# A two-layer image kernel: layer 1's pools open behind the last scan, its first steps between those of the last image's end, and the mixing made one round ahead

## The chip, the cores and the metric

The kernel runs as one launch on one core of one Trainium2 chip. The metric is the device time of the launch in microseconds (us), lower is better. Engines are called as the profile calls them: PE is TensorE (PEld its weight loads), DVE is VectorE, ACT is ScalarE, POOL is GpSimd, and SP is SyncE, which here only issues DMAs.

## The reference, cut to what matters

The input `x` is 4 images of 48 x 48 x 128 in float32. Two residual layers follow each other.

```
layer 0, per image:  xz = in_proj(group_norm(x));  xin, z = split(xz)
    xc = silu(conv3x3_depthwise(xin))                     # d = 256
    xs = [xc, xc transposed, both reversed]               # 4 directions, L = 2304
    dt, B, C = projections of xs
    h[l] = h[l-1] * exp(dt*A) + dt*u*B[l];  y[l] = h[l]*C[l]   # 16 states
    x1 = x + out_proj(layer_norm(sum of directions) * silu(z))

layer 1:  xa = instance_norm(group_norm(x1))              # (b, t): 48 x 128 pictures
    k, q, v = spectral convolutions of xa, 32 heads
    attn = softmax(q . k over t, s);  out = attn . v
    proj = spectral convolution of out + skip;  attention = inorm(proj + xa)
    m = two spectral layers of attention (gelu in the first)
    result = x1 + inorm(m) + attention
```

A spectral convolution takes the FFT of a picture, multiplies a few modes by complex weights and transforms back. The kernel does the transforms as matmuls with fixed matrices, and it works on the attention in the modes: the scores come from the transformed pictures, and the attention weights are applied to transformed pictures too ("mixing").

## The kernel before

**Two ways to place an instruction.** What is called through `on.` is kept in program order (all of it has line L55 in the profile, the line of the helper). What is called through `nc.` is placed by a scheduler on its engine, as early as its data, its memory and the order allow. Either way each engine then runs its instructions strictly in order.

**Layer 0** (`first_layer`) goes over image `b`, direction `k` in the order 0, 2, 1, 3, chunks of 480 of 2304 positions, and 16 state steps in each chunk. A step has matmuls that spread its factors (`da`, `pb`), the scan `h` on DVE, the product `hc` with the C rows `cbc` on POOL, and the matmul `yp` that sums over states. `advance` interleaves the stages of neighbouring steps; the C rows are fetched by SP four steps ahead. Everything else (projections, convolution, the end of a chunk) is written as generators in the queue `later`, of which `piece()` runs one step per `advance`. The end of a chunk is `gather`, then `back`: products `pg`, layer norm (`pm`, `yb`, `pv`, `var`, `pe`), gate (`pz0`, `pz1`, `ws`), output projection (`po`), residual (`pr`), and a store to `x1_dram`. All matmuls of `back` use one PSUM bank (`side`), so they form a serial chain. After the last step of the last image the rest of `later` runs alone:

```
    for _ in range(len(window)):
        advance(None)
    while later:
        piece()
```

**Layer 1** (`layer1`) starts when `io["first"]` has returned. It loads all four images back from `x1_dram` (`x_in`, L1000), as two pairs of images. Then:

- `prepare()` fills `qs` with zeros and builds the selection matrices `sel` (memsets and copies on POOL).
- For each pair `p`: `statistics` (`bn_stats` `st`, `mv`, and `group_affine`: `gm_l`, `gv_l`, one power `aff` on POOL), then `first_norm` (means `pm`, `po_m`; four centrings to `xa`; squares `sq`; `pv`, `po_v`; `in_r`) in turn with `forward_w`, the transform along w (`pfwb`, and six steps of two matmuls `pa` with their evacuations `a`).
- Weights of the heads: `gw` on DVE, transposes `pgt`, stored as `dgt`. Then the normalised pictures transposed (`pxn`, `xnt`), the modes of q and k selected (`psel`), and products `ps` for the modes that carry no weight (`s0`).
- Scores, per pair: twelve steps `jn` of 8 matmuls `sc` with a product `f` on DVE or POOL, then 8 matmuls `s0 . d_qk`. Beside them `keys()` makes transposed pictures, one image (48 rows) at a time: `pxt`, `xt`, stored as `dxt`. After each pair the softmax over its scores (`mx`, `s`, `sm`, `sn`), its transposes `pat` and a copy to `attn_c`.
- Mixing: 96 rounds, `k` (4) x pair (2) x `q` (3) x `g` (4). SP fetches `xrep` (two transfers of 576 KB for every four rounds, two buffers) and `grep` (576 KB, 16 in all). A round is `gp` (ACT copy, L1624), `v` on DVE (L1626), `v` on POOL (L1630) and 12 matmuls `acc` (L1634) into three PSUM banks. After twelve rounds the sums go out: one ACT copy, three DVE operations to `zt` (L1645 to L1647), and two transposes `pz` to `z2`. After the second quarter `mix_of_images` adds 24 matmuls `pa` per pair (L1570).

The rest (`Strand`, phases `p0` to `p5`, two pairs in turn) is the output projection, the two spectral layers and the result.

Of the kernel before, what the change touches and what calls it, by code (L numbers as in the profile page):

```python
# [10 lines left out]
F32 = mybir.dt.float32  # L11
# [47 lines left out]
def first_layer(ctx, tc, io, x1_dram, sp_dram, d_w, d_m):  # L59
# [14 lines left out]
    four = ctx.enter_context(tc.tile_pool(name="l0_four", bufs=4))  # L74
    ring = ctx.enter_context(tc.tile_pool(name="l0_ring", bufs=RING))
    ps_a = ctx.enter_context(tc.tile_pool(name="l0_psa", bufs=1, space=PSUM))
# [3 lines left out]
    rows = ctx.enter_context(tc.tile_pool(name="l0_rows", bufs=ROWS))  # L80
    dram = ctx.enter_context(tc.tile_pool(name="l0_dram", bufs=8, space=DRAM))

# [403 lines left out]
    def back(b, s, n, yb, x, w, wb):  # L486
# [66 lines left out]
        for f in range(NF):  # L553
            on.tensor.matmul(pr[:, 0:n], w_out[:, 1, f], z[:, f, 0:n], start=False, stop=(f == NF - 1))
        yield
        on.vector.tensor_add(xo[:, 0:n], xo[:, 0:n], pr[:, 0:n])
        last = b == B - 1 and s == 0
        (nc.scalar if last else nc.sync).dma_start(
            x1_dram[b].rearrange("w h t -> w (h t)")[:, s : s + n], xo[:, 0:n]
        )  # L560
# [313 lines left out]

    turns = deque(maxlen=2)
# [8 lines left out]
    for j, chunks in enumerate(directions):  # L884
# [3 lines left out]
        if k == ORDER[-1]:  # L888
            drain(coming)
            images[b]["x"] = load_x(b, "xr")  # L890
        nxt = upcoming(j + 1) if j + 1 < len(directions) else None
# [37 lines left out]
    while later:  # L929
        piece()  # L930
# [32 lines left out]
def layer1(ctx, tc, io, x1_dram, out):  # L963
# [11 lines left out]
    io["first"](sp_d, d_w, d_m)  # L975

    imgs = ctx.enter_context(tc.tile_pool(name="l1_imgs", bufs=1, side="right"))
    const = ctx.enter_context(tc.tile_pool(name="l1_const", bufs=1, side="right"))
    small = ctx.enter_context(tc.tile_pool(name="l1_small", bufs=2, side="right"))
    on = Ordered(tc)  # L980
    img = ctx.enter_context(tc.tile_pool(name="l1_img", bufs=1))

    def load(name, shape, src, eng=nc.sync):
        t = const.tile(shape, F32, name=name)
        eng.dma_start(t, src)
        return t
# [3 lines left out]

    xa = img.tile([128, H, BT], F32, name="xa")
    ident = load("ident1", [128, 128], io["c_ident"])
    fh = load("fh", [96, 96], io["c_FH"])
    x_in = [imgs.tile([128, 2, H, T], F32, tag=f"p{p}", name=f"x_in{p}") for p in range(2)]
    for b in range(B):

        for s, n in CHUNKS if b == B - 1 else [(0, L)]:
            h = slice(s // T, (s + n) // T)
            last = b == B - 1 and s == 0
            (nc.scalar if last else nc.sync).dma_start(x_in[b // 2][:, b % 2, h], x1_dram[b][:, h])  # L1000
    gmat = load("gmat1", [128, 128], io["c_group"])
    fw = load("fw", [128, 66], io["c_FW"])
    eps = const.tile([128, 1], F32, name="eps1")
    nc.gpsimd.memset(eps, 1e-5)
    half = const.tile([128, 1], F32, name="half1")
    nc.gpsimd.memset(half, -0.5)
    mean_m = const.tile([128, 32], F32, name="mean_m")
    nc.gpsimd.memset(mean_m, 1.0 / (H * W))
    over_h = const.tile([H, H], F32, name="over_h")
    nc.gpsimd.memset(over_h, 1.0 / H)  # L1010
    over_w = const.tile([128, T], F32, name="over_w")
    nc.gpsimd.memset(over_w, 1.0 / W)

    g_of = const.tile([128, 2, 128], F32, name="g_of")
    nc.gpsimd.memset(g_of, 0.0)
    for b in range(2):
        nc.gpsimd.memset(g_of[64 * b : 64 * b + 64, b], 1.0 / 32)
    n_g = everywhere("n_g", io["L1_norm_g"], 6)
    n_b = everywhere("n_b", io["L1_norm_b"], 6)
    HB = 8  # L1020
# [10 lines left out]
    def statistics(psum, p, x):  # L1031

        mv = small.tile([128, 2, 2], F32, tag=f"mv{p}", name=f"mv{p}", bufs=1)
        for b in range(2):
            st = small.tile([128, 6, 6], F32, tag="st", name=f"st1_{p}_{b}")
            for q in range(6):
                on.vector.bn_stats(st[:, q], x[:, b, q * HB : (q + 1) * HB].rearrange("p h t -> p (h t)"))
            on.vector.bn_aggr(mv[:, b], st)
        aff = small.tile([128, 2, 2], F32, tag=f"aff{p}", name=f"aff{p}", bufs=1)
        group_affine(on, small, psum, gmat, half, mv[:, :, 0], mv[:, :, 1], aff[:, 0], aff[:, 1], 2, f"l1{p}")  # L1040
        return aff
# [28 lines left out]
    def first_norm(psum, work, p, x, aff, y):  # L1070

        a_m = small.tile([128, 2], F32, tag="a_m", name=f"a_m{p}")
        on.vector.tensor_scalar(a_m, aff[:, 0], 1.0 / (H * W), None, ALU.mult)
        quarters = [(2 * b + i, b, 24 * i) for b in range(2) for i in range(2)]

        def spread(t, name, more=False):

            v = small.tile([128, T], F32, tag="in_s", name=f"in_{name}{p}")  # L1080
            on.vector.tensor_reduce(v, t[:, 0 : HB * T].rearrange("p (h t) -> p t h", t=T), AX.X, ALU.add)
            o = psum.tile([128, 512], F32, tag="st", name=f"po_{name}{p}", bufs=2)
            for b in range(2):
                ob = o[:, b * T : (b + 1) * T]
                on.tensor.matmul(ob, g_of[:, b], v, start=True, stop=not more)
                if more:
                    on.tensor.matmul(
                        ob, aff[:, 1, b : b + 1].to_broadcast([128, 128]), over_w, start=False, stop=True
                    )
            return o  # L1090

        pm = psum.tile([128, 512], F32, tag="st", name=f"pm{p}", bufs=2)
# [9 lines left out]
        yield  # L1102
        om = spread(pm, "m", True)
# [5 lines left out]
        yield  # L1109
        pv = psum.tile([128, 512], F32, tag="st", name=f"pv{p}", bufs=2)  # L1110
        for i, b, h in quarters:
            d = y[:, h : h + 24, p * 96 + b * T : p * 96 + (b + 1) * T]
            on.vector.scalar_tensor_tensor(
                d,
                x[:, b, h : h + 24],
                aff[:, 0, b : b + 1],
                m[:, b, None, :].to_broadcast([128, 24, T]),
                ALU.mult,
                ALU.add,
            )  # L1120
            sq = work.tile([128, 24, T], F32, tag="sq", name=f"sq{p}_{i}")
# [7 lines left out]
        ov = spread(pv, "v")  # L1129
        r = small.tile([128, 96], F32, tag=f"in_r{p}", name=f"in_r{p}", bufs=1)  # L1130
# [3 lines left out]
        yield r  # L1134

# [7 lines left out]
    a0_bd = const.tile([96, 2, 96], F32, name="a0_bd")  # L1143
    zp = ctx.enter_context(tc.tile_pool(name="l1_z", bufs=1))
# [17 lines left out]
    nc.vector.tensor_mul(wpv[:, 0], wpv[:, 0], wpv[:, 1])  # L1162
    dxt = dram.tile([B, 4, T, 3 * NC], F32, name="dxt")
# [12 lines left out]
    s0 = pe.tile([T, B, T], F32, name="s0")  # L1176
# [38 lines left out]
    def products():  # L1215
        cqk = pe.tile([T, NH], F32, name="cqk")
# [4 lines left out]
        with ExitStack() as pw:  # L1221
# [19 lines left out]
            nc.scalar.copy(n_col, pn[:, 0:4].rearrange("p (s z) -> p s z", z=2))  # L1241

# [59 lines left out]
    with ExitStack() as ph:  # L1302
        psum = ph.enter_context(tc.tile_pool(name="l1_ps0", bufs=3, space=PSUM))
        psst = ph.enter_context(tc.tile_pool(name="l1_ps0s", bufs=1, space=PSUM))
        work = ph.enter_context(tc.tile_pool(name="l1_work0", bufs=2))
        prepare()
        rs, das = [], []
        for p in range(2):
            aff = statistics(psst, p, x_in[p])
            norm = first_norm(psst, work, p, x_in[p], aff, xa)  # L1310
            trans = forward_w(psum, work, p, x_in[p], aff)
            next(norm)
            next(trans)
            next(norm)
            for _ in range(5):
                next(trans)
                next(norm)
            das.append(next(trans))
            rs.append(next(norm))
        with ExitStack() as pw:  # L1320
            ps_t = pw.enter_context(tc.tile_pool(name="l1_wt", bufs=2, space=PSUM))
            q1 = pw.enter_context(tc.tile_pool(name="l1_w1", bufs=1, side="right"))
# [4 lines left out]
            for c in range(2):  # L1327
                nc.sync.dma_start(w_p[:, :, c], io["wP"][c].rearrange("(j p) h -> p j h", p=128))
                nc.sync.dma_start(w_v[:, :, c], io["wV"][c].rearrange("(j p) h -> p j h", p=128))
                nc.sync.dma_start(d48[c], io[("c_D48r", "c_D48i")[c]])  # L1330
            for c in range(2):
                p = ps_t.tile([128, 512], F32, tag="tr", name=f"pv48{c}")
                on.tensor.matmul(p[:, 0:NH], d48[c], w_v[:, 0, c], start=True, stop=True)
                on.scalar.copy(w_v[:, 0, c], p[:, 0:NH])
            gw = q1.tile([128, 12, 3, NH], F32, name="gw")
# [14 lines left out]

            for k in range(4):
# [6 lines left out]
                nc.sync.dma_start(dgt[k], gt.rearrange("h c n -> h (c n)"))  # L1358
        pl = ph.enter_context(tc.tile_pool(name="l1_plain", bufs=1))
# [4 lines left out]
        b48 = small.tile([128, 1], F32, tag="b48", name="b48")  # L1364
        on.vector.tensor_scalar(b48, n_b[:, 0:1], 1.0 / H, None, ALU.mult)
        one1 = small.tile([1, 1], F32, tag="one1", name="one1_x")
        nc.gpsimd.memset(one1, 1.0)
        pr = psst.tile([128, 512], F32, tag="pp", name="pr0")
        r_t = small.tile([96, 2], F32, tag="r_t", name="r_t")
# [63 lines left out]
        u32 = const.tile([24, BT], F32, name="u32")  # L1433
# [783 lines left out]
```

## Time and profile before

| | |
|---|---|
| median of 3 runs | 4521.48 us (4520.93 to 4522.82) |
| profiled execution | 4536.64 us, span 4534.9 us, mean PE clock 0.936 |
| PE busy | 3854.2 us (85%) |
| DVE busy | 3854.3 us (85%) |
| ACT busy | 3439.2 us (76%) |
| POOL busy | 3356.7 us (74%) |
| layer 0, last product `hc` starts | 3709.43 us |
| end of the last chunk | 3747.4 us |
| pair 0's norm and transform, first `pm` | 3771.87 us |
| pair 1's norm and transform, first `pm` | 3808.72 us |
| scores | 3889.9 to 3993.6 us |
| mixing, first and last `acc` | 4021.8 to 4262.6 us |
| `Strand`, first matmul `pe_p` | 4269.83 us |

Starts are microseconds from the start of the span. The page divides the span into 40 slices of 113 us, each digit the busy share of an engine in tenths; PEclk is the clock that the throttle granted to PE. A line of the chain of waits is start, length, engine, operation and line, or the transfer or the "issue" time that the chain went through. In the timeline an operation's line ends with the idle time before it and what released it. The windows give, for a stretch, the busy time of PE, PEld, DVE, ACT and POOL with counts, then the PE clock, the share of the DMA engines and GB/s.

### The profile page before, as it was taken

How to read it: one execution, taken by the hardware profiler on the slowest of the kernel's cores; microseconds unless marked ns; L12 is line 12 of the kernel's file. 1: busy time of each engine (PE TensorE's matmuls, PEld its weight loads, DVE VectorE, ACT ScalarE, POOL GpSimd, SP SyncE). 2: the span in 40 equal slices, each digit the busy share in tenths (PEclk: the TensorE clock that was granted, in tenths of full speed). 3: DMA queues.
4: the chain of work that ended last, by engine and by line, in shares of the span. 5: the costliest groups of instructions: out<-in, count | busy, mean ns of one | idle time of the engine just before them, and what ended most of it. 6: DMA issues, size and time to landing. Idle time of an engine off the chain costs nothing.

```text
span 4534.9 us, 73722 instructions
## 1 busy us (share of the span) xinstructions
PE 3854.2 (85%) x26212; PEld 2993.0 (66%) x26212; DVE 3854.3 (85%) x2646; ACT 3439.2 (76%) x6964; POOL 3356.7 (74%) x3523
## 2 busy tenths in 40 slices
PE   6989987888899878888998788878877885979877
PEld 3777776777777767776777677767776762535444
DVE  3888999999899999998999999989999974657446
ACT  3888888988888889887888899879998862323344
POOL 2777788988787889887878898978888961356432
PEclk9989999999999899998999999999999997989877
DMA  2333333333333333333333333434333332155536
GB/s 63 93 94 103 91 100 100 111 96 110 97 106 94 96 102 111 98 110 94 107 93 96 103 107 100 115 94 111 104 105 105 100 111 62 25 128 138 133 101 160
DMA packets 327068, 461.05 MB, mean 102 GB/s; under 512 B 112788, under 2 KB 295636, under 8 KB 325996
## 3 DMA queue, kind: packets, MB, share of 16 engines
q1 hardware_dynamic: 311904, 433.20, 35.0%
q10 hardware_dynamic: 14796, 23.13, 1.5%
q8 instruction: 208, 3.41, 0.3%
q14 instruction: 160, 1.31, 0.1%
HBM read 400.99 MB, written 55.44 MB: 101 GB/s over the span
## 4 chain that ended last, share of the span: by engine, by line
PE 35%; ACT 22%; DVE 21%; issue 12%; POOL 5%; DMA 3%; SPq 1%; ACTq 0%; DVEq 0%; POOLq 0%
DVE h L55 13%; PE yp L55 8%; ACT scaled L55 6%; PE pc L55 5%; DVE db L55 4%; ACT da L55 4%; PE da L55 4%; ACT decay L55 4%; PE pd L55 2%; POOL hc L55 2%; PE acc L1634 2%; ACT dt L55 2%; ACT turned L55 2%; PE pg L55 2%; PE pb L55 2%
## 5 line engine op out<-in xcount | busy, mean ns | idle before, releaser
L55 POOL TENSOR_TENSOR hc<-h,cbc 128x960 f32<-128x960 f32 (+1 forms) x1280 | 2546.1, 1991 | 565.4 <-PE yp L55 194.1
L55 DVE TENSOR_TENSOR_SCAN h<-da,carry,db 128x962 f32<-128x962 f32 (+1 forms) x640 | 1355.9, 2119 | 115.7 <-ACT da L55 97.3
L55 DVE TENSOR_TENSOR_SCAN h<-decay,carry,da 128x962 f32<-128x962 f32 (+1 forms) x640 | 1362.5, 2129 | 6.5 <-PE da L55 6.2
L55 PE MATMUL yp<-ident,hc 128*128 128x128 f32 (+1 forms) x9728 | 1268.6, 283 | 52.9 <-POOL hc L55 49.3
L55 PEld LDWEIGHTS yp<-ident,hc 128*128 128x128 f32 (+1 forms) x9728 | 1140.6, 145 | 217.5 <-issue 109.3
L55 ACT ACTIVATE scaled<-turned,bt 128x256 f32<-128x256 f32 (+1 forms) x2432 | 1035.5, 497 | 27.5 <-ACT turned L55 23.6
L55 ACT ACTIVATE da<-dt,a_neg 128x480 f32<-128x480 f32 (+1 forms) x1280 | 826.1, 645 | 187.9 <-DVE h L55 165.0
L55 ACT ACTIVATE decay<-dt,a_neg 128x480 f32<-128x480 f32 (+1 forms) x1280 | 799.1, 674 | 28.2 <-DVE h L55 23.6
L55 PE MATMUL da<-ident,scaled 128*128 128x128 f32 (+1 forms) x4864 | 646.5, 276 | 194.1 <-DVE h L55 178.5
L55 DVE TENSOR_TENSOR db<-du,pb 128x960 f32<-128x960 f32 (+1 forms) x640 | 699.0, 1092 | 110.1 <-PE pb L55 100.1
L55 PEld LDWEIGHTS da<-ident,scaled 128*128 128x128 f32 (+1 forms) x4864 | 543.8, 145 | 243.0 <-ACT scaled L55 97.9
L55 PE MATMUL pb<-ident,bt 128*128 128x128 f32 (+1 forms) x2432 | 376.6, 276 | 38.4 <-DVE db L55 38.4
L55 PEld LDWEIGHTS pb<-ident,bt 128*128 128x128 f32 (+1 forms) x2432 | 292.7, 141 | 171.4 <-issue 98.2
L55 PE MATMUL pc<-pad,w_c 128*128 128x480 f32 (+1 forms) x720 | 335.9, 581 | 6.5 <-ACT th L55 3.0
L55 POOL TENSOR_TENSOR du<-dt,xc 128x480 f32<-128x480 f32 (+1 forms) x160 | 206.4, 1290 | 49.5 <-ACT dt L55 49.5
L1630 POOL TENSOR_TENSOR v<-grep,xrep 128x768 f32<-128x768 f32 x96 | 174.8, 1823 | 89.8 <-PE acc L1634 47.5
L1634 PE MATMUL acc<-v,attn_c 128*64 128x384 f32 x1152 | 211.1, 502 | 29.4 <-DVE v L1626 15.3
L1626 DVE TENSOR_TENSOR v<-gp,xrep 128x1536 f32<-128x1536 f32 x96 | 167.7, 1756 | 76.4 <-PE acc L1634 43.9
L55 PEld LDWEIGHTS da<-carry,ident 128*128 128x128 f32 x1280 | 201.6, 199 | 0.0
L55 PE MATMUL da<-carry,ident 128*128 128x2 f32 x1280 | 197.6, 224 | 0.0
L55 POOL COPY carry<-h 128x2 f32<-128x2 f32 x1024 | 194.9, 190 | 0.0
L1634 PEld LDWEIGHTS acc<-v,attn_c 128*64 128x64 f32 x1152 | 113.2, 139 | 116.8 <-issue 63.6
(382 smaller groups left out, 3995.9 us busy)
## 6 DMA issues: line engine op xcount, KB each, us to landing
cbc<-cd SPq DMA_DIRECT2D x512, 240.0 KB
cbc<-other SPq DMA_DIRECT2D x512, 240.0 KB
xrep<-dxt SPq DMA_DIRECT2D x48, 576.0 KB
cbc<-cd SPq DMA_DIRECT2D x128, 192.0 KB
cbc<-other SPq DMA_DIRECT2D x128, 192.0 KB
yt<-turned ACTq DMA_DIRECT2D x40, 384.0 KB
old<-yt SPq DMA_DIRECT2D x40, 384.0 KB
grep<-dgt SPq DMA_DIRECT2D x16, 576.0 KB
```

The costliest lines, as they stand in the source:

```text
L55: return lambda *args, **kw: self._tc.keep_in_program_order(emit(*args, **kw))
L1626: nc.vector.tensor_mul(v, gp[:, None, :, 0:NC].to_broadcast([128, 2, 2, NC]), x[:, :, 0:2])
L1630: nc.gpsimd.tensor_mul(v3, r[:, 2:3].to_broadcast([128, 2, NC]), x[:, :, 2])
L1634: nc.tensor.matmul(acc[c][64 * b : 64 * b + 64, 0:NC], attn_c[:, 2 * pair + b, g, q], v[:, b, c] if c < 2 else v3[:, b], start=first, stop ...
```

## The change

1. **Pools.** In layer 0, the pools `four`, `ring`, `rows` and `ps_a` are opened last and closed behind the last step (`scans.close()`). A new function `opening` opens layer 1's first pools there, its matmuls with one PSUM bank per tag (`pp`, `mm`, `st`).
2. **Images 0 and 1 between the steps of the end.** `return_x` loads images 0 and 1 once more into an `xc` buffer (`x_0`, eight loads of 288 KB), queued at the last image's last direction; in the built order they stand in SP's queue in image 2's last direction. Then one step of `opening` follows each piece of the last chunk's end: statistics, affine, means, transform and squares of pair 0, on `x_0`. In the built order the squares, half of the transform and the statistics of the third image come after the last piece.
3. **Last chunk's result** is added straight into `x_in[1]`, and its store goes by SP.
4. **Order behind it.** `pow` for pair 1 and its norm and transform follow; the centring of pair 0 into `xa` comes later, between the steps of the weights of the heads. `prepare()` stands later in the source; in the built order its POOL instructions stand behind the last `pv` and square of `x_0` (whose memory `qs` takes) and ahead of pair 1's `pow`. `iw2`, `fw64` and `ih` are loaded here and not after the mixing.
5. **Scores.** `keys()` takes both images of a pair (96 rows): 16 groups `pxt` in all instead of 32, all in pair 0's scores. `s0 . d_qk` comes first. The softmax is split: `open_soft` (maxima, subtraction, exponential) right behind a pair's scores; `close_soft` of pair 0 during pair 1's scores, of pair 1 around the first mixing rounds. The `xrep` of the first two steps is fetched during pair 1's scores.
6. **Mixing.** `make(n + 1)` (the copy and the products) stands before `use(n)` (the matmuls). Three ACT copies take the sums out; the DVE operations and the `pz` of a group follow in the next rounds. `grep` fetches are spread. The mix of images becomes 24 matmuls of 96 columns at the end, multiplied by a mask `own`.

The diff, cut to its core:

```diff
+    scans = ctx.enter_context(ExitStack())
+    four = scans.enter_context(tc.tile_pool(name="l0_four", bufs=4))
+    ring = scans.enter_context(tc.tile_pool(name="l0_ring", bufs=RING))
+    rows = scans.enter_context(tc.tile_pool(name="l0_rows", bufs=ROWS))
+    ps_a = scans.enter_context(tc.tile_pool(name="l0_psa", bufs=1, space=PSUM))
...
+        to = xo[:, 0:n]
+        if b == B - 1 and s == 0:
+            to = images[b]["x1"][:, 1].rearrange("w h t -> w (h t)")[:, 0:n]
+        on.vector.tensor_add(to, xo[:, 0:n], pr[:, 0:n])
+        nc.sync.dma_start(x1_dram[b].rearrange("w h t -> w (h t)")[:, s : s + n], to)
...
+    def return_x(x):
+        for i in range(NF):
+            for q in range(0, L, 576):
+                nc.sync.dma_start(x[:, i, q : q + 576], x1_dram[i].rearrange("w h t -> w (h t)")[:, q : q + 576])
+                yield FREE
...
-    while later:
-        piece()
+    scans.close()
+    with ExitStack() as tail:
+        beside = opening(tail, x_0.rearrange("p b (h t) -> p b h t", t=T), images[B - 1])
+        next(beside)
+        while later:
+            piece()
+            next(beside, None)
+        images[B - 1]["done"] = True
+        for _ in beside:
+            pass
...
+    def opening(stack, x_0, last):
...
+        measure(0, 0, x_0, range(6))
+        yield
+        measure(0, 1, x_0, range(6))
+        yield
+        made["aff"] = [affine(psum, 0)]
+        yield
+        trans = forward_w(psum, work, 0, x_0, made["aff"][0])
+        norm = means(psum, 0, x_0, made["aff"][0])
+        for _ in range(3):
+            next(norm)
+            yield
+        made["m"] = next(norm)
+        for i in range(H // HB):
+            next(trans)
+            yield
+        made["da"] = [next(trans)]
+        rest = squares(psum, None, 0, x_0, made["aff"][0], made["m"])
+        for i in range(5):
+            next(rest)
+            yield
+            if i == 1:
+                measure(1, 0, x_in[1], range(6))
+        made["r"] = [next(rest)]
+        measure(1, 1, x_in[1], range(2, 6))
...
+        while "done" not in last:
+            yield
+        measure(1, 1, x_in[1], range(2))
+        made["aff"].append(affine(psum, 1))
...
+                for _ in range(2 * (pair == 0 and jn % 3 != 2)):
+                    next(beside, None)
+                if pair and jn == 1:
+                    for i in range(2):
+                        fetch(i, ahead[:, i])
+                if pair and jn % 2 and jn < 8:
+                    close_soft(0, jn // 2)
+            for _ in beside:
+                pass
+            open_soft(pair, sc)
...
+            for g in range(4):
+                fetch_weights(0, g)
+            for g in range(2):
+                close_soft(1, g)
+            make(0)
+            for n in range(len(rounds)):
+                if n < 2:
+                    close_soft(1, 2 + n)
+                if n + 1 < len(rounds):
+                    make(n + 1)
+                todo = after.popleft() if after else None
+                use(n)
+                if todo:
+                    todo()
+                if n == len(rounds) - 12:
+                    e = weights_of_mixing()
+            mixing(e)
+            for todo in after:
+                if todo:
+                    todo()
```

## The prediction

> **What bounds the kernel now.** I read the page first: the busy tenths say where the profile is full and where it is thin.
>
> ```profile
> PE   6989987888899878888998788878877885979877
> ...
> DVE  3888999999899999998999999989999974657446
> ...
> POOL 2777788988787889887878898978888961356432
> PEclk9989999999999899998999999999999997989877
> ```
>
> Each digit is 113 us. Up to the 32nd slice (3711 us) the scan keeps TensorE (PE) and VectorE (DVE) at eight or nine tenths. Only the last seven slices have holes, and all of the diff except eight loads lies between 3711 and 4270. So the page's leading engine, 85% for PE and DVE alike, prices nothing here: each seam has its own limit.
>
> Second, the chain of waits, in order of time, for the seams:
>
> ```profile
> 3711.53 0.67 PE yp L55 x4
> ...
> 3737.98 3.58 PE po L55 x4
> ...
> 3742.30 4.42 PE pr L55 x6
> 3746.72 21.67 issue
> ...
> 3771.87 4.07 PE pm L55 x24
> ...
> 3798.72 2.78 DVE st L55 x6
> ...
> 3808.72 4.14 PE pm L55 x24
> ...
> 4008.26 11.64 DMA grep<-dgt
> ...
> 4066.11 10.68 DMA xrep<-dxt
> ```
>
> The last image's end is one serial chain from 3711.5 to 3747.4 (a 0.65 us add follows `pr`). Then nothing of layer 1 starts until the store has come back through DRAM. After that pair 0 has its statistics, norm and transform (3768 to 3798.7), and pair 1 the same, from 3798.72. At 4008 everything stands for the first weights of the mixing.
>
> Third, the timeline of GpSimd (POOL) and ScalarE (ACT), for what is queued in those seams:
>
> ```profile
> 3750.06 2.66 POOL L1174 MEMSET qs<- 128x3072 f32 x1 [12.13 <-DMA x<-ws]
> ...
> 3760.56 0.87 POOL L1213 TENSOR_TENSOR sel<-sel 96x32 f32<-96x32 f32 x4
> 3770.64 0.71 POOL L55 TENSOR_TENSOR aff<-gs_l,half 128x2 f32<-128x2 f32 x1 [9.21 <-DVE gs_l L55]
> ```
>
> ```profile
> 4017.39 0.80 ACT L1624 COPY gp<-grep 128x768 f32<-128x768 f32 x1 [10.60 <-DMA grep<-dgt]
> ```
>
> `prepare()` is 11.4 us of POOL, now in a gap. Last, busy time by stretch (PE, weight load, DVE, ACT, POOL, then clock):
>
> ```profile
> 3728.00:3747.00 19.00, 11.87 (x14) 3.91 (x14) 2.08 (x3) 2.43 (x4) 2.20 (x1) 0.53 0.24 41
> 3747.00:3771.00 24.00, 1.15 (x4) 1.00 (x4) 7.64 (x22) 0.00 (x0) 11.73 (x72) 0.55 0.11 24
> ...
> 3995.00:4020.00 25.00, 4.16 (x14) 2.30 (x16) 11.81 (x25) 4.68 (x10) 3.61 (x7) 0.57 0.55 127
> 4020.00:4263.00 243.00, 226.70 (x1304) 127.40 (x1300) 176.35 (x117) 87.19 (x119) 172.95 (x95) 0.95 0.62 144
> ```
>
> PE works 1.15 of 24 us after the tail and 4.16 of 25 before the mixing, but 227 of 243 in it.
>
> The sum is made on the profiled run: 4536.64 us, span 4534.9, hence 15.2 us above the median of 4521.48. I take the saving as the same in microseconds and subtract it from the median.
>
> **A. The tail and pair 0: −22 us (−30 to −10).** In the built order PE gets layer 1's steps between those of the tail, with one PSUM bank per tag, so each transform step waits for the evacuation of the one before. Worked forward:
> - Two statistics blocks (2.78 each) go on the idle DVE; the second follows `yb` (end 3721.6) and ends near 3724.4. Its aggregate 0.33, four small DVE operations of 0.17 and the group products 0.57 and 0.60 stand ahead of `pe`, which starts near 3727.2 instead of 3726.26: +0.9.
> - A third of `pm` (4.07/3 = 1.36) stands before `pz0`, before `pz1` and after it: together +2.1 at `pz1`.
> - `po_m` (1.09), `pfwb` (0.32) and the first two transform products (0.91, then 0.61 of evacuation, then 0.68) stand before `po`: POOL's `yb` (2.21) covers part, `po` is 4.5 late. Two more pairs, before and inside `pr`, add 3.3. The tail ends near 3755.2, +7.8.
> - Only about twelve of the opening's eighteen steps fit between pieces. Three transform pairs follow (six times 0.75 + 0.6, to about 3762.6), then on DVE four centrings of 1.34 with a 2.78 statistics block among them (to 3770.3), a square 1.17, `pv` 2.07: 3773.6.
> - A new wait: `qs` takes memory of `x_0`, so POOL's memset stands behind the last `pv` and square, and in POOL's queue all of `prepare()` (11.4, and 0.3 for a memset of `s0`) stands ahead of pair 1's 0.72 power. The power ends at 3786.0; with 0.4 for the scale and shift, `pm` of pair 1 starts near 3786.5. DVE's own chain (`in_v` 0.57, `d_qk` about 1.7, `in_r` 1.0, statistics 2.78, aggregate and group 3.3) is done at 3783, so POOL decides by 2 to 3 us.
>
> 3808.72 − 3786.5 = 22. The store round trip and pair 0's 27 us go, the tail's 7.8, the leftover 18.4 and prepare's 13 come. The loads of `wpv` and `mask` move behind the later store: 7 us to issue and 4.7 to land in the rows, so 3767.6, before DVE reads them; 6 us of cover, beyond which each microsecond counts. The `w_p` loads move too; their reader is 40 us on.
>
> The row for the clock is 0.53 in 3728 to 3747, with PE 62% busy in pieces broken by waits; 0.85 in 3771 to 3790, where it is denser. My sum keeps tail operations at their present durations. [...] I stay with the row, since the single bank keeps the pieces broken. −30 is the lower end if the tail runs like the 0.85 row; −10 if the moved steps wait a further evacuation each (18 × 0.6).
>
> **B. Pair 1's norm and transform up to the projections: 0 (−3 to +4).** The same instructions (28 us). The four centrings for `xa` of pair 0 (4 × 1.34) come later on DVE, beside 12 us of PE transposes (`pgt`); uncovered they cost 5.4.
>
> **C. Scores and softmax: −31 (−38 to −18).**
> - Pair 0: `s0·d_qk` (2.06) is issued first, while PE now waits 3.44 for the first `f`: −2.
> - Between pairs PE stops 8.4 us (3936.5 to 3944.9). Only maxima and subtractions (8 × 0.5) remain before the bank is free: −4.
> - Pair 1: its 16 `pxt` groups (0.75 each, 12 us) go, since one group now does 96 rows; four `pat` (0.9) of pair 0 come. 47.8 → about 39.8: −8. DVE holds 8 × 3.44 + 4 × 1.6 = 34 here and stays covered.
> - From the last score (3992.8) to the first mixing product (4021.8) is 29 us. Now `xrep` is there, DVE has 4 us of maxima and subtractions, two closings (1.5 each) and `v` (1.76), and the first `grep` has 2.6 for a transfer's latency and 2.5 for 576 KB at the 230 GB/s seen: first product after about 10: −19. Three more `grep` at 2.5 each feed rounds that want 2.0: +2.
>
> **D. Mixing, 96 rounds: −20 (−34 to −4).** Undisturbed, 128 `acc` records take 21.53, twelve to a round: 2.02 a round. The eight groups end 25.5, 31.2, 28.7, 34.4, 33.7, 29.9, 30.1 and 27.3 apart; the last is undisturbed: 24.2 of rounds, 1.2 of `pz`, about 2 of PE waiting for `zt` and the next `v` behind it. With one round made ahead and ACT copying the sums, I take 1.7 off at seven ends: −12. `pa` (2 × 4.2) leaves: −8.4. Of the remaining 16 us of DMA stalls I count nothing saved: 12 `xrep` and 4 `grep` per quarter are 9.4 MB, 41 us at 230 GB/s out of 48 of rounds, and `xrep` still has two buffers. −34 if all the stalls go; −4 if the waits for transfers widen as much as the ends shrink.
>
> **E. End of the mixing: −1 (−4 to +3).** `ih` is loaded early, but 24 new products (4.21/48 each, so 2.1; double if the wider ones run slower) stand ahead of `pz`.
>
> **The scan: +1 (0 to +5).** Eight loads of 288 KB go into SP's queue in image 2's last direction among the 240 KB state loads: 10 us of transfer at 230 GB/s, in a stage at about 100 GB/s, with state rows fetched four steps ahead.
>
> Sum: −22 − 31 − 20 − 1 + 1 = −73; 4521.5 − 73 = 4448.5, say 4449 us.
>
> **Rivals.**
> *The seams close less* (0.19). The tail is paced by evacuations (A −15), the weights arrive with the fetches in each other's way (C −22), the DMA stalls take the mixing's gain (D −6): −42 with the rest, 4480. For it: 10.68 us waits for `xrep`; against: PE was 93% busy there anyway.
> *PE's floor is reached* (0.15). A −28, C −36, D −32, E −3: −99, 4422. For it: the last group at 27.3; against: the DMA share of 0.62 with bursts over 1.0.
> *Slower: the round loses its overlap* (0.10). `make(n+1)` stands before `use(n)` with two `v` buffers. If a `v` can only be made after the products of the round before it, a round is 1.68 + 2.02 = 3.7 and not 2.02: 96 × 3.7 = 355 against 241, +114 on gains of 53 elsewhere: +61, 4582. It decides from 3.1 us a round on. Against it: two buffers carry 2.02 a round already.
>
> **How the numbers follow.** My forecast, 4449 (4432 to 4466), has 0.56. The range runs from 4420 to 4487: it takes in nearly all of the first two rivals and leaves the slower one out. 0.2% (9 us) is about what a measurement can tell from no change. 0.02 of the first rival lies within it: faster 0.88, same 0.02, slower 0.10.
>
> **What would show it.** Right: no `issue` stretch of 20 us after `pr`; `pr` ends near 3754; POOL's `qs` memset starts near 3773 and pair 1's `pm` near 3786; 8 to 11 us from last score to first `acc`; groups of 25 to 28 us. Wrong in A: `pm` of pair 1 after 3798, or one released by DVE and not POOL. Wrong in D: groups as long as now, or ended by `xrep`. Wrong altogether: a span above 4526.

## The result, and the profile after

The changed kernel takes 4457.41 us (median of 4 runs, 4451.84 to 4459.33) against 4522.15 us beside it (4520.93 to 4529.98): a ratio of 0.9851, 95% interval 0.9834 to 0.9868, or 65 us less. The forecast was 4449 us with a range from 4420 to 4487. The profiled execution has a span of 4457.0 us, 77.9 less than before's. That difference is larger because the execution of before that was profiled lay 14.5 us above its median, the one of after only 1.4 us.

The busy tenths of the page (a slice is now 111 us, so the slices do not match one to one):

```profile
PE   6989987888899978898999788878887796989866
...
DVE  3989899999898999998999999998999995578546
...
POOL 2777788988787889887778898887888984258432
PEclk9999999999899999998999999999999998999987
```

The thin part still begins at the 33rd or 34th slice, but it is fuller: PE's 5 there has become a 6, and the mixing's slices stand at 8 and 9. The tenths ahead of it are those of before within one.

Now the timeline around the last image's end, from the POOL, DVE and PE answers (start, length, engine, line, operation, and in brackets the idle time before it with its releaser):

```profile
3707.39 2.05 POOL L55 TENSOR_TENSOR hc<-h,cbc 128x960 f32<-128x960 f32 x1 [0.62 <-issue]
...
3772.31 2.66 POOL L1250 MEMSET qs<- 128x3072 f32 x1 [33.57 <-PE pv L55]
...
3783.92 0.69 POOL L55 TENSOR_TENSOR aff<-gs_l,half 128x2 f32<-128x2 f32 x1
```

```profile
3753.99 0.64 DVE L55 TENSOR_TENSOR x_in<-ws,pr 128x480 f32<-128x480 f32 x1
...
3781.68 0.16 DVE L55 TENSOR_SCALAR gs_l<-gv_l 128x2 f32<-128x2 f32 x1 [0.68 <-PE gv_l L55]
3784.65 0.16 DVE L55 TENSOR_TENSOR aff<-gmean_l,aff 128x2 f32<-128x2 f32 x1 [2.81 <-POOL aff L55]
```

```profile
3732.93 1.07 PE L55 MATMUL pz<-xp,w 128*128 128x480 f32 x2
...
3750.30 0.86 PE L55 MATMUL pa<-x,fwa 128*66 128x384 f32 x2 [0.71 <-DVE a L55]
3751.00 1.77 PE L55 MATMUL pr<-ws,w_out 128*128 128x480 f32 x4
...
3785.14 4.14 PE L55 MATMUL pm<-x_in,a_m 128*32 128x384 f32 x24 [3.50 <-DVE a_m L55]
```

The 21.67 us of "issue" behind `pr` are gone. The tail ends at 3754.6, later than before. POOL's `qs` waits for `pv`, `prepare()` follows, and pair 1's power comes behind it: DVE has its input ready at 3781.84, POOL takes it at 3783.92.

The chain of waits for the mixing:

```profile
3965.61 1.82 POOL v L1753
3967.48 1.54 PE acc L1769 x2
...
4015.87 8.53 DMA grep<-dgt
...
4042.81 6.96 DMA xrep<-dxt
...
4077.00 11.44 DMA xrep<-dxt
...
4097.04 6.86 DMA xrep<-dxt
...
4171.72 15.63 PE acc L1769 x96
4187.35 4.25 PE pa L1712 x48
```

The wait before the first `acc` is short now. Inside, `xrep` and `grep` still appear, and at the end eight rounds run undisturbed in 15.63 us, 1.95 a round.

Stage by stage, each from the two profiled executions:

| stage | before | after | difference | forecast |
|---|---|---|---|---|
| start of the last `hc` | 3709.4 | 3707.4 | -2.0 | +1 |
| from there to the first `pm` of pair 1 | 99.3 | 77.8 | -21.5 | -22 |
| to the end of `ps` | 76.9 | 78.8 | +1.9 | 0 |
| to the last score | 109.3 | 96.4 | -12.9 | -14 |
| to the first `acc` | 24.4 | 7.2 | -17.2 | -17 |
| to the last `acc` | 243.9 | 219.9 | -24.0 | -20 |
| to the first `pe_p` | 6.6 | 7.6 | +1.0 | -1 |
| to the end | 265.1 | 262.1 | -3.0 | 0 |

The first `acc` of before starts at 4019.4 us by the trace, and its last score ends at 3995.0 and its last `acc` at 4263.3; the table counts from these. The 4021.8 in the table of before, which the prediction also uses, is the start of the third pair of records.

### The profile page after: what moved, and what is told of

It reads as the page before. It is cut to its first block, busy times and chain, and to the rows that moved or that the text cites. A ratio compares the mean times of both kernels' runs of the same rounds, so it can differ in the third digit from the quotient of the medians.

```text
span 4457.0 us, 73318 instructions
## 1 busy us (share of the span) xinstructions
PE 3808.3 (85%) x26040; PEld 2932.0 (66%) x26040; DVE 3865.2 (87%) x2652; ACT 3440.9 (77%) x6963; POOL 3351.2 (75%) x3515
## 5 line engine op out<-in xcount | busy, mean ns | idle before, releaser
L1753 POOL TENSOR_TENSOR v<-grep,xrep 128x768 f32<-128x768 f32 x88 | 162.7, 1852 | 35.1 <-PE acc L1769 23.3
L55 PE MATMUL pd<-xd,w_dt 40*128 40x480 f32 (+1 forms) x320 | 172.1, 619 | 16.7 <-ACT bt L55 7.8
L1751 DVE TENSOR_TENSOR v<-gp,xrep 128x1536 f32<-128x1536 f32 x88 | 153.7, 1754 | 27.6 <-PE acc L1769 12.4
```

Source lines behind the costliest of these rows:

```text
L55: return lambda *args, **kw: self._tc.keep_in_program_order(emit(*args, **kw))
L1751: nc.vector.tensor_mul(v, gp[:, None, :, 0:NC].to_broadcast([128, 2, 2, NC]), x[:, :, 0:2])
L1753: nc.gpsimd.tensor_mul(v3, r[:, 2:3].to_broadcast([128, 2, NC]), x[:, :, 2])
```

## Experiments

The stages of every run, from its profile, in us. "last hc" is its end; "tail" and "pm" count from there to the end of the last chunk and to pair 1's first `pm`; the others are counted as in the table above. Times are medians, the ratio is to the kernel before in the same job.

| run | last hc | tail | pm | to ps | scores | to acc | mixing | time | ratio, 95% interval |
|---|---|---|---|---|---|---|---|---|---|
| before | 3711.5 | 35.9 | 97.2 | 76.9 | 109.3 | 24.4 | 243.9 | 4522.2 | |
| changed | 3709.4 | 45.2 | 75.7 | 78.8 | 96.4 | 7.2 | 219.9 | 4457.4 | 0.9851 [0.9834, 0.9868] |
| not made ahead | 3688.0 | 46.4 | 76.6 | 77.6 | 96.9 | 7.1 | 220.5 | 4455.1 | 0.9855 [0.9836, 0.9874] |
| fetch late in the source | 3703.7 | 46.4 | 76.6 | 77.6 | 96.9 | 7.1 | 218.9 | 4452.5 | 0.9844 [0.9828, 0.9861] |
| tail alone | 3703.4 | 34.6 | 105.8 | 79.2 | 96.9 | 7.0 | 218.4 | 4483.3 | 0.9913 [0.9898, 0.9928] |
| sums by DVE | 3711.8 | 46.2 | 76.2 | 77.6 | 96.4 | 7.3 | 225.2 | 4461.8 | 0.9844 [0.9824, 0.9864] |
| first xrep in the pool | 3713.9 | 46.4 | 76.6 | 77.6 | 96.9 | 12.6 | 220.4 | 4457.9 | 0.9828 [0.9802, 0.9853] |
| half of xrep | 3697.2 | 45.2 | 75.7 | 78.7 | 96.5 | 6.9 | 213.1 | 4441.8 | 0.9799 [0.9778, 0.9820] |
| three xrep | 3691.2 | 46.1 | 76.2 | 77.6 | 96.4 | 7.1 | 238.0 | 4474.5 | 0.9868 [0.9841, 0.9895] |
| two banks | 3704.1 | 43.2 | 71.3 | 77.7 | 96.1 | 6.9 | 219.1 | 4438.1 | 0.9812 [0.9781, 0.9842] |
| four edits | 3699.0 | 42.5 | 71.5 | 77.2 | 96.3 | 11.9 | 226.6 | 4462.7 | 0.9859 [0.9838, 0.9880] |
| changed, again | 3702.5 | 45.3 | 75.4 | 77.6 | 96.5 | 7.3 | 221.8 | 4451.4 | 0.9834 [0.9809, 0.9859] |
| power first | 3712.4 | 42.0 | 68.5 | 80.4 | 95.8 | 6.9 | 219.8 | 4448.0 | 0.9818 [0.9795, 0.9841] |
| two banks, again | 3698.0 | 43.8 | 71.8 | 77.7 | 96.5 | 6.9 | 219.1 | 4447.3 | 0.9815 [0.9792, 0.9839] |

Stages repeat within about 1 to 3 us, whole times within about 10. So causes are read from the stages. Each edit below is on the changed kernel.

**Rounds not made ahead.**

```diff
-            make(0)
             for n in range(len(rounds)):
...
-                if n + 1 < len(rounds):
-                    make(n + 1)
+                make(n)
```

> The changed kernel with one thing undone: each round of the mixing is made just before it is used, not one round ahead. In the changed kernel the mixing takes 219.9 us from first to last acc (240.8 before). Theory: the round made ahead is what hides the ends of the groups; undone, seven ends cost about 1.7 us each again, so the mixing takes about 232 us and the time is about 12 us more (4469). Rival: the gain of the mixing came from the 48 pa matmuls that left its middle (8.4 us), from the copies by ACT and from the spread fetches; then the mixing stays within 3 us of 219.9.

The mixing took 220.5 us against 219.9. The rival holds, but for a reason of its own: `make` and `use` are placed by the scheduler, and in the built order SP and POOL run the same sequence as the changed kernel and PE, DVE and ACT differ in a handful of rows at the first closings. Writing the round ahead in the source moved nothing.

**First xrep fetched behind the scores, in the source.**

```diff
-                    if pair and jn == 1:
-                        for i in range(2):
-                            fetch(i, ahead[:, i])
...
                 open_soft(pair, sc)
+                if pair:
+                    for i in range(2):
+                        fetch(i, ahead[:, i])
```

> The changed kernel, but the xrep of the first two steps is fetched behind the last scores and not during pair 1's scores. In the changed kernel 7.1 us lie between the last score and the first acc (29.1 before). Theory: the early fetch carries much of that; four transfers of 576 KB at 230 GB/s are 10 us and share the engines with the first grep, so the gap becomes 14 to 18 us and the time 7 to 11 us more. Rival: the gap shrank because the softmax was split and the DVE chain sets it; then it stays at 9 us or less and the time within 2 us.

7.1 us, as if nothing had been done, and in the built order nothing was: all five engines run the same sequence. It does not decide between the two; as a run it is a repeat of the changed kernel (4452.5 us).

**First xrep in the mixing's own buffers**, so that memory keeps the fetch back.

```diff
-                        ahead = zp.tile([128, 2, 2, 3, NC], F32, tag="z96", name="ahead")
...
+            fetch_x(0)
             for g in range(4):
                 fetch_weights(0, g)
```

> The changed kernel, but the xrep of the first two steps goes into the mixing's own buffers, whose memory comes free only behind the last scores (this time the order of SP does change: the four transfers stand behind the last score). Theory: the early fetch carries part of the 22 us gained between the last score and the first acc; now two xrep and one grep of 576 KB stand in front of the first v: 2.6 + 3 x 2.5 + 1.8 is 12 us instead of 7.1, and the later grep are late too, so the time is 5 to 9 us more. Rival: the softmax's split set the gap; it stays at 8 us or less.

12.6 us instead of 7.2: the theory's 12. So the early fetch carries 5.4 us of the 17 gained in that gap. The other 12 are left to the split softmax and the earlier weights by difference alone; no run undid those. The time (4457.9) does not show 5 us.

**The tail alone.**

```diff
         while later:
             piece()
-            next(beside, None)
```

> The changed kernel, but the last image's end runs alone and the steps of the opening all follow it. From the start of the last hc to the last chunk's end takes 46.6 us in the changed kernel, and pair 1's first pm starts 77.8 us after that hc. Theory: the steps between the pieces delay the end by 8 to 9 us but take about 26 us of work off what follows; undone, the end is back at 37 to 38 us, and pm of pair 1 comes about 18 us later (95 to 97 us after hc), the time 15 to 18 us more. Rival: with one PSUM bank the interleaving costs as much as it hides; then pm of pair 1 stays within 4 us.

The timeline of DVE and PE in this run:

```profile
3737.41 0.65 DVE L55 TENSOR_TENSOR x_in<-ws,pr 128x480 f32<-128x480 f32 x1 [2.83 <-PE pr L55]
3737.98 5.61 DVE L55 BATCH_NORM_STATS2 st<-x 128x6 f32<-128x384 f32 x12
...
3750.39 0.16 DVE L1292 TENSOR_TENSOR wpv<-wpv 128x4 f32<-128x4 f32 x1 [4.98 <-DMA mask<-in_c_ident]
```

```profile
3809.22 3.50 PE L55 MATMUL pm<-x_in,a_m 128*32 128x384 f32 x20 [3.40 <-DVE a_m L55]
```

The tail is back at 34.6 us (theory: its old length; the gap to 45.2 is the 10 us that the interleaving costs it), and `pm` of pair 1 comes 30 us later, with 26 us in the time (4483.3; 28 and 31 over the two repeats of the same job). Of the 30, 5 are a side effect: DVE now reaches the `wpv` product before its `mask` has landed and stands 4.98 us. Another 7 are PE's clock. The twelve `pa` have the same waits of 0.7 us as in the changed kernel, but they take 1.5 us each, where most take 0.86 in the changed kernel, and the granted clock from 3760 to 3786 was 0.50:

```profile
3764.74 1.54 PE L55 MATMUL pa<-x,fwa 128*66 128x384 f32 x2 [0.73 <-ACT a L55]
```

So interleaving is worth about 25 us net, 18 of them without the clock, and 18 were expected. Without it nothing of A is left: `pm` at 105.8 is later than before's 97.2.

**Sums by DVE.**

```diff
-                for c in range(3):
-                    nc.scalar.copy(s[:, c], acc[c][:, 0:NC])
+                nc.scalar.copy(s[:, 0], acc[0][:, 0:NC])
+                t2, t3 = acc[1], acc[2]
...
-                after.extend((combine, lambda: turn_over(0), None, lambda: turn_over(1)))
+                combine()
+                turn_over(0)
+                turn_over(1)
```

> The changed kernel, but a group of the mixing ends as before the change: one ACT copy, three DVE operations that read the other two sums in PSUM, and the transposes at once. The run with rounds not made ahead in the source left the mixing at 220 us, so that is not what hides the ends. Theory: the three ACT copies free the banks early and let v go first; undone, DVE's first v of a group again waits behind zt, about 1.7 us at seven ends, and the mixing takes 229 to 234 us instead of 219.9, the time 9 to 14 us more. Rival: the ends were cheap, and the gain was the 48 pa that left; then the mixing stays within 3 us of 219.9.

225.2 us: 5.3 more, between the two expectations. At the end of a group `zt` now reads PSUM and `v` stands 1.9 us for PE, as it did before the change (DVE's timeline of this run):

```profile
4001.58 0.56 DVE L1789 TENSOR_TENSOR zt<-acc,s 128x384 f32<-128x384 f32 x1
4004.04 1.76 DVE L1751 TENSOR_TENSOR v<-gp,xrep 128x1536 f32<-128x1536 f32 x1 [1.91 <-PE acc L1769]
```

So the group ends were worth 0.75 us each at seven ends, not 1.7.

**Half of xrep.** `fetch` takes only the first image's rows, and the products use them for both.

```diff
-            for b in range(2):
+            for b in range(1):
                 s = b * T + q * 16
```

> The changed kernel with half of the xrep transfers left out: both images of a pair use the rows of the first (that part of the result is another one). Theory: the waits for xrep in the mixing's chain are transfer time on two buffers; with half the bytes they go, and the mixing takes 205 to 211 us instead of 219.9. Rival: PE and POOL, at 2.0 and 1.93 us a round, are the limit; the mixing stays at 216 us or more.

213.1 us, 6.8 less: the rival's 216 is missed, and the theory's 205 to 211 is not reached. PE's waits within the mixing come to 0.8 us, against 8 in the changed kernel. So transfers still cost the mixing 7 us.

**Three xrep.**

```diff
-            px = ph.enter_context(tc.tile_pool(name="l1_qx", bufs=2))
+            px = ph.enter_context(tc.tile_pool(name="l1_qx", bufs=3))
...
-            pg = ph.enter_context(tc.tile_pool(name="l1_qg", bufs=6))
+            pg = ph.enter_context(tc.tile_pool(name="l1_qg", bufs=5))
...
-                if g == 0 and i != 2 and i + 1 < len(steps):
-                    fetch_x(i + 1 + (i < 2))
+                if g == 0 and i + 2 < len(steps):
+                    fetch_x(i + 2)
```

> The changed kernel with three xrep buffers instead of two, fetched two steps ahead; to make room the grep buffers are five instead of six (grep fetched right as a buffer comes free) and the sums are combined in place. Theory: the transfer waits are waits for a free buffer, so the mixing falls from 219.9 to 205 to 212 us, the time by 8 to 15. Rival: 9.4 MB a quarter at 230 GB/s are the limit, or grep with one buffer less becomes late; the mixing stays at 216 us or more.

The room is short: six `grep` buffers take 27 KB of a partition, and beside three `xrep` 19.7 are left; hence five, and the sums in place.

238.0 us, 18 more. The waits of ACT, DVE and POOL for transfers, and of PE for the sums, from 3968 to 4160 us, changed kernel first, then this one (engine, line, waited for, us in total, times, longest):

```profile
ACT gp L1749 <- DMA grep<-dgt: 7.4, 6, 2.5
DVE v L1751 <- DMA xrep<-dxt: 6.9, 7, 2.6
POOL v L1753 <- DMA xrep<-dxt: 5.4, 3, 3.1
```

```profile
ACT gp L1746 <- DMA grep<-dgt: 21.1, 9, 4.7
PE pz L1789 <- DVE zt L1783: 8.8, 5, 2.0
PE acc L1766 <- ACT zt L1778: 8.3, 4, 2.3
```

The `xrep` waits are gone; for `grep`, with one buffer less and behind the next `xrep` in SP's queue, ACT waits three times as long, and its copies of the sums come late behind it. That is the rival's second half. But the sums in place have a price of their own: over the whole mixing PE waits 22.6 us against 8 in the changed kernel, and 10.8 of them are for `zt` ahead of `pz`, a wait that the changed kernel does not have. So the run does not price the third buffer alone.

**Two banks** for `pa` of images 0 and 1.

```diff
+        psmm = stack.enter_context(tc.tile_pool(name="l1_psm", bufs=2, space=PSUM))
...
-        trans = forward_w(psum, work, 0, x_0, made["aff"][0])
+        trans = forward_w(psmm, work, 0, x_0, made["aff"][0])
```

> The changed kernel with two PSUM banks instead of one for the transform products pa of images 0 and 1. In the changed kernel each pa waits about 0.7 us for the evacuation of the one before, the tail takes 45 us from the last hc's end and pair 1's first pm starts 75.7 us after it. Theory: the single bank is what paces the steps between and behind the pieces; with two, five to eight of the twelve waits go, the tail is 2 to 4 us shorter and pm of pair 1 comes 4 to 6 us earlier (70 to 72). Rival: the chain goes through DVE (centring, statistics, squares) and POOL's prepare behind it; pm of pair 1 stays within 1.5 us.

`pm` of pair 1 at 71.3 us instead of 75.7, the tail 2 us shorter: the theory, with its numbers. PE's timeline shows the waits gone, six products `pa` (two records each) in 4.71 us that took about 9:

```profile
3745.29 4.71 PE L55 MATMUL pa<-x,fwa 128*66 128x384 f32 x12
```

**Four edits together:** two banks, the power ahead of `prepare` (its operations kept in program order), pair 0's centrings inside pair 1's stage, and three xrep with fetches kept in program order.

> The changed kernel with four edits that the runs point to: pair 1's power on POOL ahead of prepare (minus 2 us), pair 0's centrings for xa inside pair 1's stage (minus 2 to 4 us before the scores), two banks for pa, and three xrep with five grep buffers, this time with the fetches kept in program order, so that grep stands ahead of the xrep two steps on. Theory: with grep no longer late the mixing takes 208 to 213 us instead of 219.9 (half the xrep bytes gave 213.1), and the whole is 12 to 20 us shorter than the changed kernel. Rival: transfers at 230 GB/s stay the limit in the mixing, which keeps at 218 us or more, and the whole gains 4 to 8 us.

The whole gained nothing: 4462.7 us. `pm` of pair 1 gained nothing over two banks (71.5), the centrings at most 0.5 us, and the mixing took 226.6 us. The `grep` waits of ACT fell to 5.5 us, but fetches in strict order put the gap before the mixing at 11.9 us, and PE waits for the sums, which are combined in place here too:

```profile
PE pz L1793 <- DVE zt L1787: 12.3, 7, 1.9
```

Less these 12.3 the mixing would stand at some 214 us, an estimate just above the theory's 208 to 213. Whether a third `xrep` pays with the sums kept apart was not settled. Why the power did not help, the two timelines show (DVE, then POOL):

```profile
3767.11 0.16 DVE L55 TENSOR_TENSOR aff<-gmean_l,aff 128x2 f32<-128x2 f32 x1 [0.81 <-POOL aff L55]
3767.30 3.12 DVE L55 TENSOR_SCALAR aff<-aff 128x2 f32<-128x2 f32 x1
```

```profile
3766.38 0.69 POOL L55 TENSOR_TENSOR aff<-gs_l,half 128x2 f32<-128x2 f32 x1 [38.83 <-DVE gs_l L55]
3767.03 2.66 POOL L55 MEMSET qs<- 128x3072 f32 x1
```

**Power first,** with the long memset at the end of `prepare`, and two banks; and **two banks, again.**

```diff
-    nc.gpsimd.memset(qs, 0.0)
...
+        on.gpsimd.memset(qs, 0.0)
     def products():
```

> The changed kernel with two banks for pa (pm of pair 1 71.3 us after the last hc) and pair 1's power ahead of prepare on POOL, this time with the long memset of qs (2.66 us) at prepare's end. In the run with all four edits the power came 2 us earlier, but the three small tensor_scalar operations of DVE behind it (0.16 us each elsewhere) stood 3.1 us, until the memset that POOL had begun was over, and pm of pair 1 came no earlier (71.5). Theory: DVE was held by POOL's instruction; with only short memsets behind the power those operations take at most 0.5 us each and pm of pair 1 comes at 68 to 69.5. Rival: the short ones hold DVE as long in sum; pm of pair 1 stays at 71 or more. In the time 2 us cannot be told (it is 0.05%).

> The changed kernel with two banks for pa once more, beside the version with the power first. pm of pair 1 at 71 to 71.5 us after the last hc, the tail at 43 us; the time 4 us less than the changed kernel's, within what its executions differ.

`pm` of pair 1 at 68.5 us, within the theory's 68 to 69.5, and DVE's operation behind the power takes 0.53 us:

```profile
3780.28 0.53 DVE L55 TENSOR_SCALAR aff<-aff 128x2 f32<-128x2 f32 x1
```

But "to ps" grew to 80.4, so up to the end of `ps` the two stand at 148.9 and 149.5 us. The products `psel` give the gain back: they start 3.9 us earlier than in two banks, again, and then 158 records of them take 3.3 us longer (power first, then two banks again):

```profile
3841.85 9.96 PE L1519 MATMUL psel<-a_x,sel 96*32 96x192 f32 x158
```

```profile
3831.32 6.70 PE L1519 MATMUL psel<-a_x,sel 96*32 96x192 f32 x158
```

PE is busy without a break in both; the granted clock was 0.50 in the one's 3842 to 3848 us and 1.00 in the other's 3828 to 3834. Whether the edit brings this or only the execution that was profiled is open. Two banks again: 71.8 us and 4447.3 us, its ratio 0.9815 beside 0.9812. No version with the full result was faster, though power first, at 0.9818, cannot be told from it. The stage shows some 4 us over the changed kernel; the intervals of the times overlap.

**The changed kernel again.**

> The changed kernel once more, beside the two others. Stages as before: tail 45 to 46.5 us, pm of pair 1 75.7 to 76.6 us after the end of the last hc, mixing 218.5 to 220.5; what varies between its executions is the scan (the last hc's end has been seen from 3688 to 3714 us with the same instructions in it) and the last stage (262 to 271).

All as expected (45.3, 75.4; the mixing 221.8, 1.3 above), 4451.4 us.

## Why the prediction was right

**A, right in sum and mechanism.** 21.5 us against 22. The tail grew by 9.3 (forecast 7.8), `qs` started at 3772.3 (3773.6), the power ended at 3784.6 (3786.0), `pm` began at 3785.1 (3786.5): all about 1.5 us early after a scan that ended 2.0 early. POOL decided by 2.1 us, as forecast. The row of the clock, 0.53, did not hold for the whole tail: the windows of after are

```profile
3728.00:3747.00 19.00, 14.82 (x50) 4.77 (x48) 3.56 (x8) 3.72 (x7) 2.21 (x1) 0.69 0.05 12
3747.00:3764.00 17.00, 9.81 (x24) 2.92 (x24) 7.47 (x12) 2.88 (x5) 0.00 (x0) 0.99 0.19 56
```

The clock was 0.69 and 0.99 where before had 0.53. `pz1` fell from 1.97 to 1.07 and `pr` from 4.42 to 2.74, at a granted clock of 1.00 (0.50 and 0.60 in before), while `pz0` stayed at 1.97 and `po` at 3.41, at 0.50 as in before. Why the clock rose for these two and not for the others was not shown.

Yet the tail grew by more than the row's sum, which kept all four at their old lengths. The term that was too small is the first: `pe` was to start 0.9 us late, and starts 2.9 late, counted from the last `hc`'s end (17.7 against 14.8 us). In POOL's queue pair 0's power stands ahead of the tail's `var`, and the sum did not have it (after, then before):

```profile
3725.43 0.70 POOL L55 TENSOR_TENSOR aff<-gs_l,half 128x2 f32<-128x2 f32 x1 [13.84 <-DVE gs_l L55]
3726.10 1.02 POOL L55 TENSOR_TENSOR var<-var,half 128x4 f32<-128x4 f32 x1
```

```profile
3725.19 1.01 POOL L55 TENSOR_TENSOR var<-var,half 128x4 f32<-128x4 f32 x1 [11.38 <-ACT var L55]
```

These 2.0 us, and 2.1 more in the steps after `pe`, outweighed the 2.6 that the clock gave. So that 9.3 came near 7.8 is in part luck. The single bank's share is known: a second one returned 2 us in the tail and 4.4 to `pm`. The list of what goes and comes also leaves out pair 1's statistics, 10 us of DVE and PE in before, which now run beside `prepare()`; the times that it subtracts contain them. The run with the tail alone shows that this interleaving, and not the round trip through DRAM alone, carries A.

**B, right within its bounds.** 1.9 us against 0 (to +4). The centrings of pair 0 were nearly covered: they are 5.40 us of DVE from 3819.25, and PE's first `pxn` of that stage waits 0.19 us for `xa`. The repeats have 77.6, +0.7. The other 1.2 belong to the execution: its granted clock was 0.57 from 3828 to 3836, and 1.00 at that place (3823 to 3831) in the run with the fetch late in the source.

**C, right in sum, less in its parts.** 30.1 us against 31. Pair 0's scores gave 4.3 (forecast 2). Between the pairs only 0.8 came instead of 4 (PE's pause went from 7.3 to 6.6 us): the first `f` of pair 1 (1.76) stands on DVE ahead of the first maximum, which the sum had not seen. Pair 1 gave 7.8 (8), and the gap before the first `acc` 17.2 (19 less 2). The base of that last term was read too long: the 29 us run to the third pair of records of `acc`, and from the end of the last score to the first `acc` it was 24.4. The gap came to 7.2, where about 10 was forecast.

**D, right in sum, with its terms mis-sized.** 24.0 us against 20. The term "1.7 off at seven ends, 12" measured 5.3 when it was undone. The 48 `pa` that left were 8.4 by their rows. Two groups of the page show where the rest lies (before, then after; busy time, mean of one in ns, idle time before):

```profile
L1634 PE MATMUL acc<-v,attn_c 128*64 128x384 f32 x1152 | 211.1, 502 | 29.4 <-DVE v L1626 15.3
```

```profile
L1769 PE MATMUL acc<-v,attn_c 128*64 128x384 f32 x1152 | 203.0, 492 | 9.1 <-DVE v L1751 5.4
```

Without the wait ahead of the first `acc` (13.1 and 1.0) PE's waits fell from 16.3 to 8.1 us. And the same 1152 products were busy 8.1 us less, a term that the sum put at nothing: the granted clock within the mixing was 0.95 before and 0.99 after. That the shorter waits are the reason for the clock was not shown. Of the waits that are left, half of `xrep` takes away nearly all. And the step "with one round made ahead" named the wrong cause: the scheduler had the same order without it. That 20 came near 24 is in part luck: a term twice too large met one that was left out.

**E and the rest.** +1.0 against -1, within its bounds: the 24 products take 4.25 us ahead of `pz`, the upper of the two prices. The last stage, not touched, was 3.0 us shorter, and over the runs it lies between 257 and 271, so no effect of the change can be read from it. The loads of `x_0` (forecast +1) cannot be seen: the last `hc` ended between 3688 and 3714 us in kernels with the same instructions in the scan.

**The rivals.** The round did not lose its overlap: 96 rounds at 2.3 us with all ends, and 1.95 in the last eight. PE's floor was not reached (219.9 against 243.9 less 32). The first rival had 15, 22 and 6 us for A, C and D, where 21.5, 30.1 and 24.0 were measured; it was right only in that the mixing still waits for transfers.

## What to carry to other kernels

A serial tail on one engine's short operations is a place for the next layer's first steps, and the price is set by the buffers they turn in: here the tail grew by 9 us, some 25 came back net, 7 of them by PE's granted clock (0.99, and 0.50 with the tail alone), and a second PSUM bank gave 4 more. Before a source order is credited with a gain, look at the order that was built: two edits here moved nothing, because a scheduler places those instructions. When a wait is taken off one engine, look at what the freed engine starts next; in the run with four edits POOL began a memset of 2.66 us, and DVE's operation behind the power took 3.12 us instead of 0.17: 2.95 us more, where the wait for the power had been 2.81 us in the changed kernel.

## What the runs showed of the hardware

DVE's `tensor_scalar` on 128 x 2 elements, 0.16 to 0.17 us elsewhere, took 3.12 us in the run with four edits while POOL ran a memset of 2.66 us that had begun 0.27 us earlier, and 0.53 us in the run with the power first, beside four short memsets of 0.53 us together (the long wait ended 0.73 us after the memset, which others had followed at once); a `tensor_tensor` of the same size, issued 0.08 us into the same memset, took its 0.16. So two elements a partition were enough to be held. Why the one form was held and the other was not, no run shows.

The products `pa`, with the same waits of about 0.7 us between them, ran at a granted clock of 0.99 in the changed kernel (3747 to 3764 us) and of 0.50 in the run with the tail alone (3760 to 3786). So the share of time in which PE is busy, 58% and 70%, does not tell here which clock is granted. What PE did before differs, 78% busy in the one (3728 to 3747) and 37% in the other (3740 to 3760); that this decides was not shown.

The scan, with the same instructions in the same order, ended anywhere from 3688.0 to 3713.9 us in thirteen profiles of the changed kernel and its variants, while a stage such as the mixing repeats within about 3. Causes of a few microseconds are thus lost in the whole time.
